# Cross-attention in two layers: the scores move to the head of a slot, and everything that prepares them is issued one slot earlier

## The chip, the cores and the metric

The kernel runs on one core of a Trainium2 chip. The metric is the device time of one execution in microseconds, as the median over several executions. A core has five engines that work side by side and meet through semaphores: TensorE (PE in the profile, with its weight loads on a row of their own, PEld), VectorE (DVE), ScalarE (ACT), GpSimd (POOL), and SyncE (SP), which here issues nearly all DMA transfers. Matrix products land in PSUM, which has 8 banks.

## The reference

Two layers of cross-attention run one after the other over `x` of shape (32, 256, 320), with a context of 77 tokens of width 512 for each of the 32 examples. There are 20 heads of width 16. The reference also has projections for further context tokens, but the context has exactly the 77 text tokens, so those parts work on nothing. For each layer what remains is:

```python
q = heads(x @ Wq)              # 32 x 20 x 256 x 16
k = heads(ctx @ Wk)            # 32 x 20 x 77 x 16
v = heads(ctx @ Wv)
s = einsum('bhqd,bhkd->bhqk', q, k) / sqrt(16)
p = softmax(s, axis=-1)
out = merge(einsum('bhqk,bhkd->bhqd', p, v))
x = out @ Wo + bo + x          # the second layer starts from this x
```

All of it is in float32.

## The kernel before

**Units and groups.** Two examples make a pair `p` (16 pairs). A pair in one layer is a unit `u` (32 units; `units_in_order` puts four pairs of layer 0 first and then alternates the layers). The 320 channels of a unit are handled in five groups `g` (`NG = 5`), each with four pairs of heads. `x`, `q` and the output are kept with channels on partitions and the rows of the example along the free axis.

**The steps of a unit.** `load_x` and `load_context` fetch the inputs through SP. `keys` and `keys_rest` project the context (psk) and GpSimd spreads the result over two masked copies, `kT`, of which `maxima` reads. `queries` and `queries_rest` project x (psq); ScalarE copies the result out of PSUM, and SP copies `q0` to `q1`. `vals` projects a chunk of 128 context tokens (psv), and `place_vals` sends the rows by DMA to where a unit's `v` is wanted.

The softmax needs a maximum over the 77 keys for each query and head. `maxima(u, g)` (line 335, PSUM tiles psm) computes the products with queries on partitions, and VectorE reduces each of the four tiles (line 343, about 0.44 us each). When all five groups are done, `turn(u)` transposes the maxima (line 352) and sends them with eight small DMAs into spare rows of q0 and q1 (line 356). `scores(u, g)` (line 369, tiles pss) computes the products a second time with keys on partitions; the spare rows and `kM` subtract the maximum in the same matmul. ScalarE then takes the exponential of each of the four tiles into `pT` (line 375). `values(u, g)` multiplies `pT` with `v` (line 389, tile po), VectorE transposes the result (line 401), takes the reciprocal of the sums (line 405), GpSimd multiplies (line 410), and `turn_back` transposes into `oT` (line 424). `finish` and `finish_rest` project the five groups of `oT` with Wo (tiles psy) and add bias and x (line 431). In `finish`, the products over the first 256 channels, that is groups 0 to 3, come first (`main_channels`), those over the last 64, group 4, at the end (`last_channels`).

**The order of the work.** There is no scheduler: the order on each engine is the order in which the Python code issues the steps. The loop near line 462 places every step in a numbered slot. A unit starts its scores at slot `s = 5 u`, with one group per slot, so `scores(u, g)` stands in slot `s + g` and `values(u, g)` in slot `s + g + 1`. All other steps stand at fixed distances from `s`. Within a slot the steps are issued by kind, in the order of the tuple in line 506:

```python
order = ("load", "maxima", "turn", "scores", "values", "rest", "back", "full", "last")
```

So a slot in the middle of the run holds the maxima of one group of a later unit, the scores of one group of the present unit, the values of the group before, and one or two projections ("rest", "full", "last"). With 32 units there are 160 slots that hold scores. Every engine works through its part of that list strictly in this order, apart from weight loads, which can go ahead of matmuls.

**PSUM.** All tiles in PSUM come from one pool of eight banks with one tag (`bank`, line 103), handed out in turn: the ninth tile asked for gets the bank of the first. The first instruction that writes a tile waits until the last reader of the tile that had the bank eight places earlier is done. Maxima and scores ask for four banks each, values for one, `queries` and `finish` for four each, and the other projections for one or two.

Of the kernel before, what the change touches and what calls it, by code (L numbers as in the profile page):

```python
# [60 lines left out]
NG = 5  # L61
# [29 lines left out]
def xattn_kernel(ctx: ExitStack, tc: tile.TileContext, xT, cT, cP, weights, outT):  # L91
    nc = tc.nc
# [10 lines left out]
    def bank(name):  # L103
        return psum.tile([P, 512], F32, tag="bank", name=name)
# [3 lines left out]
    def load_x(p):  # L108
        x_sb = io.tile([P, NX], F32, tag="x", name=f"x_{p}", bufs=AHEAD + 3)
        nc.sync.dma_start(out=x_sb, in_=xT[p])  # L110
        xs[p] = x_sb

    def load_context(u):
        p = units[u][0]
        c_sb = cs[u] = io.tile([P, NKA, NB * L], F32, tag="c", name=f"c_{u}", bufs=3)
        nc.sync.dma_start(out=c_sb, in_=cP[:, p])
# [10 lines left out]
    def load_weights(layer, first, last, queue):  # L127
        a = PARTS[first][0]
        at, rows, width = PARTS[last]
        b = at + rows * width  # L130
        queue.dma_start(out=w_sb[layer]["all"][:, a:b], in_=weights[layer][:, a:b])
# [12 lines left out]
    for layer in range(2):  # L144
        for i in range(2):

            v = const.tile([P, HEADS // 2, 2, 2, HD], F32, name=f"stage_{layer}_{i}")
# [82 lines left out]
    def keys(u):  # L230
        p, layer = units[u]
        w, c_sb = w_sb[layer], cs[u]
        kR = st[u]["kr"] = work.tile([P, NG, L], F32, tag="kR", name=f"kR_{u}", bufs=2)
        st[u]["k"] = work.tile([P, 2, NG, L], F32, tag="kT", name=f"kT_{u}", bufs=3)
        for t in range(2):
            ps = bank(f"psk_{u}_{t}")
            for kc in range(NKA):
                by_columns(
                    ps[:, 0 : 2 * L],
                    w["k"][:, kc, t * P : (t + 1) * P],  # L240
                    c_sb[:, kc, :],
                    start=(kc == 0),
                    stop=(kc == NKA - 1),
                )
            nc.scalar.copy(kR[:, 2 * t : 2 * t + 2].rearrange("p g k -> p (g k)"), ps[:, 0 : 2 * L])  # L245
        mask_keys(u, 0, 4)

    def keys_rest(u):

        p, layer = units[u]  # L250
        w, c_sb = w_sb[layer], cs[u]
        ps = bank(f"psk_{u}_2")
        for kc in range(NKA):
            for i in range(4):
                b, m = i // 2, i % 2
                nc.tensor.matmul(  # L256
                    ps[32 * i : 32 * i + 32, 0:L],
                    w["k"][:, kc, 2 * P + 32 * m : 2 * P + 32 * m + 32],
                    c_sb[:, kc, b * L : (b + 1) * L],
                    start=(kc == 0),  # L260
                    stop=(kc == NKA - 1),
                )
        nc.scalar.copy(st[u]["kr"][:, 4], ps[:, 0:L])
        mask_keys(u, 4, 5)

    def queries(u):
        p, layer = units[u]
        w = w_sb[layer]
        q0, _ = st[u]["q"] = [
            work.tile([P, NX], F32, tag=f"q{e}", name=f"q{e}_{u}", bufs=3) for e in range(2)  # L270
        ]
        ps = [[bank(f"psq_{u}_{t}_{b}") for b in range(NB)] for t in range(2)]
        last_channels(ps, w["q2"], xs[p], start=True, stop=False)
        main_channels(ps, w["q"], xs[p], start=False, stop=True)
        for g in range(4):
            nc.scalar.copy(of_group(q0, g), ps[g // 2][g % 2][:, 0:S])  # L276

    def queries_rest(u):
        p, layer = units[u]
        w = w_sb[layer]  # L280
        q0, q1 = st[u]["q"]
        ps = bank(f"psq_{u}_2")
        project_rest(ps, w["q"], w["q22"], xs[p])
        nc.scalar.copy(of_group(q0, 4), ps[:, 0:S])
        nc.sync.dma_start(out=q1, in_=q0)
        less_keys(u)
# [41 lines left out]
    def maxima(u, g):  # L328
        q0, kT, mx = st[u]["q"][0], st[u]["k"], maxes[u % 2]
        q = of_group(q0, g)  # L330
        ps = [bank(f"psm_{u}_{g}_{j}") for j in range(4)]
        for c in range(S // P):
            for j in range(4):
                r = slice(32 * j, 32 * j + 32)
                nc.tensor.matmul(  # L335
                    ps[j][:, c * 2 * L : (c + 1) * 2 * L],
                    q[r, c * P : (c + 1) * P],
                    kT[r, :, g, :],
                    start=True,
                    stop=True,  # L340
                )
        for j in range(4):
            nc.vector.tensor_reduce(  # L343
                mx[:, 2 * g : 2 * g + 2, 2 * j : 2 * j + 2],
                ps[j][:, : 4 * L].rearrange("p (c e k) -> p c e k", e=2, k=L),
                AX.X,
                ALU.max,
            )

    def turn(u):  # L350
        mT = work.tile([P, 2 * NG * 32], F32, tag="mT", name=f"mT_{u}", bufs=2)
        nc.vector.transpose(mT, maxes[u % 2].rearrange("p k i -> p (k i)"))
        for e in range(2):
            q = st[u]["q"][e].rearrange("(j i) n -> i j n", i=32)[HD * (1 - e)]
            for a in range(P // 32):
                nc.sync.dma_start(  # L356
                    out=q.rearrange("j (k a n) -> a j k n", a=P // 32, n=32)[a],
                    in_=mT[32 * a + e : 32 * a + 8 : 2].rearrange("j (k n) -> j k n", n=32),
                )
# [77 lines left out]
    def finish(u):  # L437
        w = w_sb[units[u][1]]
        ps = [[bank(f"psy_{u}_{t}_{b}") for b in range(NB)] for t in range(2)]
        main_channels(ps, w["o"], st[u]["o"], start=True, stop=False)  # L440
        last_channels(ps, w["o2"], st[u]["o"], start=False, stop=True)
        for g in range(4):
            add(u, g, ps[g // 2][g % 2])

    def finish_rest(u):
        p, layer = units[u]
        w = w_sb[layer]
        ps = bank(f"psy_{u}_2")
        project_rest(ps, w["o"], w["o22"], st[u]["o"])
        add(u, 4, ps)  # L450
        if layer == 1 and u < NU - 1:
            nc.sync.dma_start(out=outT[p], in_=xs[p])
        st[u].clear()
# [4 lines left out]
    def at(slot, where, step):  # L458
        place.setdefault((slot, where), []).append(step)

    made = [0, 0]
    for u, (p, layer) in enumerate(units):
        s = NG * u
        if layer == 0 and u > 0:
            at(s - 14, "load", lambda p=p: load_x(p))
        if u > 0:
            at(s - 12, "load", lambda u=u: load_context(u))
        at(s - 8 if u else s - 9, "rest", lambda u=u: keys(u))
        at(s - 9, "last", lambda u=u: queries(u))
        at(s - 7, "rest", lambda u=u: keys_rest(u))  # L470
        need = range(p * NB * L // P, ((p + 1) * NB * L - 1) // P + 1)
        when = s - 6
        for i in need:
            if i < made[layer]:
                at(when, "full", lambda u=u, i=i: place_vals(u, i))
                continue
            at(when - 3, "load", lambda layer=layer, i=i: load_chunk(layer, i))
            at(when, "full", lambda layer=layer, i=i: vals(layer, i))
            at(when, "full", lambda u=u, i=i: place_vals(u, i))
            made[layer] += 1  # L480
            when = s - 5
        at(s - 5, "rest", lambda u=u: queries_rest(u))
        for g in range(NG):
            at(s - 6 + g, "maxima", lambda u=u, g=g: maxima(u, g))
            at(s + g, "scores", lambda u=u, g=g: scores(u, g))
            at(s + g + 1, "values", lambda u=u, g=g: values(u, g))
            at(s + g + 1, "back", lambda u=u, g=g: turn_back(u, g))
        at(s - 2, "turn", lambda u=u: turn(u))
        if u < NU - 2:
            at(s + NG + 1, "full", lambda u=u: finish(u))  # L490
            at(s + NG + 3, "rest", lambda u=u: finish_rest(u))
        else:

            slot = NG * NU - (u == NU - 2)
            at(slot, "full", lambda u=u: finish(u))
            at(slot, "last", lambda u=u: finish_rest(u))


    at(-10, "load", lambda: load_weights(0, "v", "v", nc.scalar))
    at(-4, "load", lambda: load_weights(0, "o", "b", nc.sync))  # L500
    at(1, "load", lambda: load_weights(1, "k", "k", nc.sync))
    at(2, "load", lambda: load_weights(1, "q", "q22", nc.sync))
    at(3, "load", lambda: load_weights(1, "v", "v", nc.sync))
    at(4, "load", lambda: load_weights(1, "o", "b", nc.sync))

    order = ("load", "maxima", "turn", "scores", "values", "rest", "back", "full", "last")
    for slot in range(min(s for s, _ in place), max(s for s, _ in place) + 1):
        for where in order:
            for step in place.get((slot, where), ()):
# [96 lines left out]
```

## Time and profile before

| | |
|---|---|
| median of 3 runs | 984.96 us (984.57 to 988.63) |
| profiled execution, its own time | 986.19 us |
| its span, from the first to the last instruction | 984.4 us |
| granted TensorE clock, mean | 0.995 |
| busy: TensorE | 968.2 us |
| busy: VectorE, ScalarE, GpSimd | 566.7, 430.1, 240.9 us |

A timeline row gives the start in us from the start of the span, the time from the first start to the last end, engine, line and operation, the tile written and the tiles read, the shapes, and how many instructions were merged into the row. In brackets stands how long the engine was idle before it and what ended that. Rows of matmuls overlap: the end of a matmul is modelled, so distances are read from start to start. TensorE shows two records for each float32 matmul of the program, so the 8 matmuls of a group of maxima, scores or values are 16 records. "Idle before" on the row of weight loads (PEld) is not idle time of TensorE, which may be busy with matmuls meanwhile.

### The profile page before, as it was taken

The page shows a single profiled execution, that of the slowest core. Times are in us where ns is not written, and L with a number is a line of the kernel's source. Part 1 is how long each engine was busy: PE and PEld are TensorE (multiplying, and loading weights), DVE is VectorE, ACT ScalarE, POOL GpSimd, SP SyncE. Part 2 cuts the span into 40 slices and gives each one's busy share as a digit, 9 for nine tenths or more (in the row PEclk, how much of TensorE's full clock was granted, in tenths as well). Part 3 has the DMA queues.
Part 4 walks back from the last instruction along what each step waited for, and adds up shares of the span by engine and source line. Part 5 has one row for each costly group of instructions (what it writes and reads, how often), then busy time and mean ns, then how long its engine had stood idle before and what let it go on. Part 6 is the DMA issues. An engine that isn't in the chain of part 4 may idle for free.

```text
span 984.4 us, 43943 instructions
## 1 busy us (share of the span) xinstructions
PE 968.2 (98%) x19664; PEld 597.3 (61%) x19664; DVE 566.7 (58%) x1316; ACT 430.1 (44%) x937; POOL 240.9 (24%) x364
## 2 busy tenths in 40 slices
PE   7899999999999999999999999999999999999988
PEld 4566665666665666665666666666656666656644
DVE  2466555665555655556655556655556655556554
ACT  1354444444444444444544444543444444444443
POOL 3132221322212322212312213322223222123211
PEclk9999999999999999999999999999999999999999
DMA  6450222212132311323212232311323122231111
GB/s 216 165 174 21 92 80 97 70 62 72 64 123 71 121 54 50 107 81 123 63 51 85 70 124 71 104 44 60 123 81 118 33 67 70 70 108 48 50 57 55
DMA packets 53949, 83.59 MB, mean 85 GB/s; under 512 B 15556, under 2 KB 35652, under 8 KB 53762
## 3 DMA queue, kind: packets, MB, share of 16 engines
q1 hardware_dynamic: 53330, 78.96, 24.0%
q8 instruction: 154, 2.52, 1.0%
q10 hardware_dynamic: 432, 1.84, 0.5%
q14 instruction: 33, 0.27, 0.1%
HBM read 35.39 MB, written 10.49 MB: 47 GB/s over the span
## 4 chain that ended last, share of the span: by engine, by line
PE 97%; DMA 1%; DVE 1%; SPq 1%; POOL 0%; issue 0%; ACT 0%; DVEq 0%; POOLq 0%
PE po L389 16%; PE psy L173 15%; PE psq L173 15%; PE pss L369 14%; PE psm L335 12%; PE psv L173 9%; PE psk L173 7%; PE psq L212 4%; PE psy L212 4%; PE psk L256 2%; SPq L356 1%; DMA w<-in_w_dram 1%; DVE max L343 0%; DMA q<-mT 0%; POOL kT L219 0%
## 5 line engine op out<-in xcount | busy, mean ns | idle before, releaser
L375 ACT ACTIVATE pT<-pss 77x512 f32<-77x512 f32 x640 | 326.8, 590 | 210.4 <-PE pss L369 210.4
L343 DVE TENSOR_REDUCE max<-psm 128x4 f32<-128x308 f32 x640 | 260.6, 469 | 197.4 <-PE psm L335 194.0
L410 POOL TENSOR_TENSOR normal<-turned,inv 128x256 f32<-128x256 f32 x160 | 99.2, 620 | 684.5 <-DVE inv L405 684.5
L369 PE MATMUL pss<-q,kM 32*77 32x256 f32 x2560 | 170.9, 377 | 4.5 <-DMA q<-mT 4.5
L389 PE MATMUL po<-pT,v 77*32 77x256 f32 x2560 | 173.1, 388 | 1.3 <-DVE max L343 1.3
L173 PE MATMUL psy<-oT,w 128*32 128x256 f32 (+1 forms) x3072 | 149.2, 380 | 0.0
L173 PE MATMUL psq<-x,w 128*32 128x256 f32 (+1 forms) x3072 | 149.2, 379 | 0.0
L276 ACT COPY q<-psq 128x256 f32<-128x256 f32 x128 | 47.6, 372 | 205.9 <-PE psq L173 202.1
L401 DVE STREAM_TRANSPOSE turned<-po 128x512 f32<-128x512 f32 x160 | 113.3, 708 | 38.4 <-PE po L389 35.4
L424 DVE STREAM_TRANSPOSE oT<-normal 128x256 f32<-128x256 f32 x160 | 71.3, 445 | 109.4 <-POOL normal L410 109.4
L335 PE MATMUL psm<-kT,q 32*128 32x154 f32 x2560 | 129.4, 314 | 1.2 <-POOL kT L219 1.2
L335 PEld LDWEIGHTS psm<-kT,q 32*128 32x128 f32 x2560 | 92.2, 183 | 57.0 <-issue 34.9
L389 PEld LDWEIGHTS po<-pT,v 77*32 77x32 f32 x2560 | 67.4, 109 | 89.9 <-DVE max L343 58.7
L173 PEld LDWEIGHTS psq<-x,w 128*32 128x32 f32 (+1 forms) x3072 | 85.4, 108 | 57.2 <-issue 13.6
L173 PEld LDWEIGHTS psy<-oT,w 128*32 128x32 f32 (+1 forms) x3072 | 82.2, 109 | 61.2 <-issue 13.2
L369 PEld LDWEIGHTS pss<-q,kM 32*77 32x77 f32 x2560 | 102.2, 142 | 24.5 <-issue 6.8
L219 POOL TENSOR_SCALAR kT<-kR,masks 128x77 f32<-128x77 f32 (+1 forms) x128 | 96.7, 766 | 50.9 <-ACT kR L245 41.3
L431 DVE SCALAR_TENSOR_TENSOR x<-psy,w,x 128x256 f32<-128x256 f32 x160 | 68.6, 479 | 61.2 <-PE psy L173 56.5
L173 PE MATMUL psv<-w,cv 128*32 128x320 f32 x1232 | 93.5, 433 | 0.0
L173 PE MATMUL psk<-c,w 128*32 128x154 f32 x2048 | 75.0, 298 | 5.8 <-DMA w<-in_w_dram 5.8
L173 PEld LDWEIGHTS psk<-c,w 128*32 128x32 f32 x2048 | 67.0, 111 | 12.9 <-DMA w<-in_w_dram 5.8
L173 PEld LDWEIGHTS psv<-w,cv 128*32 128x32 f32 x1232 | 41.1, 110 | 40.6 <-issue 2.2
(25 smaller groups left out, 349.1 us busy)
## 6 DMA issues: line engine op xcount, KB each, us to landing
q<-q SPq DMA_DIRECT2D x32, 640.0 KB
x<-in_xT_dram SPq DMA_DIRECT2D x16, 640.0 KB
c<-in_cP_dram SPq DMA_DIRECT2D x32, 308.0 KB
cv<-in_cT_dram SPq DMA_DIRECT2D x38, 256.0 KB
out_dram<-x SPq DMA_DIRECT2D x15, 640.0 KB
v<-stage SPq DMA_DIRECT2D x26, 192.5 KB
q<-mT SPq DMA_DIRECT2D x256, 5.0 KB
w<-in_w_dram ACTq DMA_DIRECT2D x2, 640.0 KB
```

What stands on the lines that cost most here:

```text
L173: nc.tensor.matmul(out[m : m + 32], lhsT[:, m : m + 32], rhs, **flags)
L212: nc.tensor.matmul(ps[r, 0:S], lhsT, rhs, start=(kc == 0), stop=(kc == 2))
L219: nc.gpsimd.tensor_scalar_mul(kT[:, e, g0:g1], kR[:, g0:g1], masks[:, e : e + 1])
L335: nc.tensor.matmul(ps[j][:, c * 2 * L : (c + 1) * 2 * L], q[r, c * P : (c + 1) * P], kT[r, :, g, :], start=True, stop=True,)
L343: nc.vector.tensor_reduce(mx[:, 2 * g : 2 * g + 2, 2 * j : 2 * j + 2], ps[j][:, : 4 * L].rearrange("p (c e k) -> p c e k", e=2, k=L), AX.X ...
L369: nc.tensor.matmul(ps[j][:L, e * S : (e + 1) * S], kM[r, e, g, :], q[r, :], start=True, stop=True,)
L375: nc.scalar.activation(st[u]["p", g][j][:L], ps[j][:L], AF.Exp, scale=SCALE)
L389: nc.tensor.matmul(po[32 * j : 32 * j + 32, e * S : (e + 1) * S], vpad[:L, b, pair, e].rearrange("p a d -> p (a d)"), pT[j][:L, e * S : (e ...
L401: nc.vector.transpose(turned[:, 0 : 2 * S], po)
L410: nc.gpsimd.tensor_tensor(normal.rearrange("p q e d -> p e q d"), outs, inv.unsqueeze(3).broadcast_to([P, 2, S // 32, HD]), ALU.mult,)
L424: nc.vector.transpose(of_group(st[u]["o"], g), normal)
L431: nc.vector.scalar_tensor_tensor(x, ps[:, 0:S], w_sb[layer]["b"][:, 0, t : t + 1], x, ALU.add, ALU.add)
```

## The change

Two things are changed. In a slot, scores are now issued first, ahead of the maxima and `turn`. And every step that prepares scores (loads, keys, queries, vals, maxima, `turn`) and `finish` of the units up to the last two is placed one slot earlier relative to the scores and values. Steps that prepare scores keep their distances among themselves; `finish(u)` moves from the slot after the unit's last values into the same slot, behind them and behind their `turn_back`. The two last units' `finish` stays where it was.

```diff
     for u, (p, layer) in enumerate(units):
         s = NG * u
         if layer == 0 and u > 0:
-            at(s - 14, "load", lambda p=p: load_x(p))
+            at(s - 15, "load", lambda p=p: load_x(p))
         if u > 0:
-            at(s - 12, "load", lambda u=u: load_context(u))
-        at(s - 8 if u else s - 9, "rest", lambda u=u: keys(u))
-        at(s - 9, "last", lambda u=u: queries(u))
-        at(s - 7, "rest", lambda u=u: keys_rest(u))
+            at(s - 13, "load", lambda u=u: load_context(u))
+        at(s - 9 if u else s - 10, "rest", lambda u=u: keys(u))
+        at(s - 10, "last", lambda u=u: queries(u))
+        at(s - 8, "rest", lambda u=u: keys_rest(u))
         need = range(p * NB * L // P, ((p + 1) * NB * L - 1) // P + 1)
-        when = s - 6
+        when = s - 7
...
-            when = s - 5
-        at(s - 5, "rest", lambda u=u: queries_rest(u))
+            when = s - 6
+        at(s - 6, "rest", lambda u=u: queries_rest(u))
         for g in range(NG):
-            at(s - 6 + g, "maxima", lambda u=u, g=g: maxima(u, g))
+            at(s - 7 + g, "maxima", lambda u=u, g=g: maxima(u, g))
             at(s + g, "scores", lambda u=u, g=g: scores(u, g))
             at(s + g + 1, "values", lambda u=u, g=g: values(u, g))
             at(s + g + 1, "back", lambda u=u, g=g: turn_back(u, g))
-        at(s - 2, "turn", lambda u=u: turn(u))
+        at(s - 3, "turn", lambda u=u: turn(u))
         if u < NU - 2:
-            at(s + NG + 1, "full", lambda u=u: finish(u))
-            at(s + NG + 3, "rest", lambda u=u: finish_rest(u))
+            at(s + NG, "full", lambda u=u: finish(u))
+            at(s + NG + 2, "rest", lambda u=u: finish_rest(u))
...
-    at(-10, "load", lambda: load_weights(0, "v", "v", nc.scalar))
-    at(-4, "load", lambda: load_weights(0, "o", "b", nc.sync))
+    at(-11, "load", lambda: load_weights(0, "v", "v", nc.scalar))
+    at(-5, "load", lambda: load_weights(0, "o", "b", nc.sync))
...
-    order = ("load", "maxima", "turn", "scores", "values", "rest", "back", "full", "last")
+    order = ("load", "scores", "maxima", "turn", "values", "rest", "back", "full", "last")
```

The chunk loads stand three slots ahead of `when` and move with it.

## The prediction

> **What bounds the kernel now.** I read the page first: busy times, then the chain that ended last.
>
> ```profile
> span 984.4 us, 43943 instructions
> PE 968.2 (98%) x19664; PEld 597.3 (61%) x19664; DVE 566.7 (58%) x1316; ACT 430.1 (44%) x937; POOL 240.9 (24%) x364
> PE 97%; DMA 1%; DVE 1%; SPq 1%; POOL 0%; issue 0%; ACT 0%; DVEq 0%; POOLq 0%
> ```
>
> TensorE is the bound, and the table of stages says how completely: from 100 to 900 us it is busy for 800.00 of 800.00 us at clock 1.00. So in the steady part there is no idle time to win. All that an order can do there is leave TensorE idle. What can be won lies in the first 45 and the last 45 us.
>
> Second, the timeline of one steady slot, TensorE alone, then ScalarE.
>
> ```profile
> 422.64 0.81 PE L335 MATMUL psm<-kT,q 32*128 32x154 f32 x16
> 423.27 1.07 PE L369 MATMUL pss<-q,kM 32*77 32x256 f32 x16
> 424.27 1.07 PE L389 MATMUL po<-pT,v 77*32 77x256 f32 x16
> 425.15 1.48 PE L212 MATMUL psq<-x,w 128*32 128x256 f32 x24
> 426.56 0.81 PE L335 MATMUL psm<-kT,q 32*128 32x154 f32 x16
> ```
>
> Read the starts, since ends overlap: maxima (M) to scores (S) 0.63 us, S to values (V) 1.00 here (0.97 in most slots: 418.51 to 419.48), V to the projection 0.88, that one to the next M 1.41. Nothing is late. From M to V takes 1.60 us.
>
> Third, who waits for whom around V and around the exponentials.
>
> ```profile
> L375 ACT ACTIVATE pT<-pss x640: 582/592/598, 40.2 to 968.8; 77x512 f32<-77x512 f32 x160
> ...
> 424.39 2.04 ACT L375 ACTIVATE pT<-pss 77x512 f32<-77x512 f32 x4 [1.18 <-PE pss L369]
> ```
>
> Four exponentials follow each S: the first starts 1.12 us after S (423.27 to 424.39) and takes 0.59, the others 0.5 apart. V of this slot reads exponentials of the slot before, so today nobody in the slot needs them soon.
>
> Last, both ends of the run.
>
> ```profile
> 37.30 0.67 PE L369 MATMUL pss<-q,kM 32*77 32x256 f32 x8 [0.23 <-DMA q<-mT]
> 39.55 0.67 PE L369 MATMUL pss<-q,kM 32*77 32x256 f32 x8 [1.57 <-DMA q<-mT]
> 40.15 2.79 PE L212 MATMUL psq<-x,w 128*32 128x256 f32 x24
> ...
> 952.95 0.67 PE L369 MATMUL pss<-q,kM 32*77 32x256 f32 x8 [1.00 <-DMA q<-mT]
> 955.35 1.15 PE L369 MATMUL pss<-q,kM 32*77 32x256 f32 x8 [1.72 <-DMA q<-mT]
> 956.42 1.93 PE L389 MATMUL po<-pT,v 77*32 77x256 f32 x16
> ```
>
> Here scores wait for the maxima that `turn` sends by DMA, and the rows after the wait run slowly (2.79 us where the same 24 take 1.48 at 425.15): the granted clock is 0.78 from 36.2 to 43.8 us and 0.80 from 944.7 to 962.
>
> **The change, part by part.** No instruction is added or removed: projections, loads, maxima, `turn` and `finish` keep their order among themselves, and S and V come one slot later against all of them. In a slot the order M, S, V, projection becomes S, M, V, projection.
>
> *The bank that V takes.* All PSUM tiles come from one ring of 8 banks. In a slot M takes 4, S takes 4 and V is the ninth, so V takes the first bank of whichever came first. Before, that is M's first bank, released by VectorE's first maximum (0.44 us long). After, it is S's first bank, released by ScalarE's first exponential of the same slot. The waits in the program of the changed kernel say so: V's first matmul waits for ScalarE alone, at the count that this slot's first exponential sets, in each of the 152 slots (1 to 152) that hold S, M and V. S and M share slots 0 to 152; slot 0 has no V.
>
> Price, from S's start. S now follows a projection, V or `finish` instead of M. The rows for that are in the tail: S at 949.85 behind the projection at 948.44 (gap 1.41, as for M, so the start of a slot does not move), first exponential at 951.03, that is 1.18 (S behind M: 1.12). With 0.59 it ends at 1.77. Handing a bank back costs about 0.06: the maximum at 60.15 takes 0.44, and V's weights start at 60.65. So V starts at 1.83. Without the wait it could start earlier: S to the next operation takes 1.03 at most (949.85 to 950.88, where V follows), M to a 128-row operation 0.74 (14.90 to 15.64), together 1.77 at most, so the exponential comes last either way. Against 1.60 before, each slot gets 0.23 longer: 152 x 0.23 = **35.0 us**. Bounds: with 1.12 as S has it behind M, 0.17 a slot, 25 us; with 1.18 and as much again as the 0.06 of the handover, 0.29 a slot, 44 us. I take 0.23, because S in the new place has the tail's neighbours. V's own length (0.88) and the projection behind it stay; its first bank is S's second, whose exponential ends 0.5 after the first, 2.33 after S, while it starts at 1.83 + 0.88 = 2.71: hidden by V.
>
> *What is queued behind the wait.* On TensorE everything. On VectorE: the maxima start 0.82 after M, so about 1.74 after S (M 0.92 after S, by S's own pitch), and end at 3.4, then transpose 0.72, reciprocal 0.25, GpSimd's multiply 0.62 with about 0.2 of handing over, transpose back 0.45, ending near 5.6. A slot lasts at least 2.71 + 1.41 = 4.12, so the next maximum is wanted at 5.9 or later: nothing is late. `turn` (0.51) and the last add of `finish_rest` (0.48) fall into one slot of about 4.7 us. `turn` pushes the chain to 6.2, the add fits while GpSimd multiplies, and the next maximum is wanted at 6.4: zero, with 0.1 x 32 = 3 us as the upper end.
>
> *`finish` one slot earlier against V.* It now follows V of its own unit's last group and needs that group's output only in its last 16 matmuls, which begin 3.57 us after its first (399.69 to 403.26). It starts at 2.71, they begin at 6.28, the output is there at 5.6 to 5.7. Cost 0, by a cover of 0.6 us; were it gone by as much again, 30 x 0.6 = 18 us.
>
> *Loads and queues.* x, context and chunk loads, the weights, the placing of v, the copies q1 and the 8 transfers of each `turn` all move together, so SP's order changes only around `out` and nothing of it is waited for in the steady part (TensorE has no DMA wait between 45 and 940 us). GpSimd's masks (2.08, 0.94, 1.31 us) keep their places against the projections; the multiply behind them comes later in the slot, not earlier. 0.
>
> *Both ends.* Between the first `turn` and the first S there is now a whole slot more: M, the rest of the queries (1.41) and S, instead of M and S. S's first half starts near 38.4, its second waits from 38.9 to 39.55 for the DMA: 0.65 in place of 0.23 + 1.57, and without the slow stretch (1.3 us in the 24 matmuls, 0.3 behind them, 0.4 ahead of S). Gain 3.2, at least 1.2 if the clock drops all the same. In the tail one pair S and V (2.0 us) moves into the time that is waited for the last `turn`; by hand I get the last half of S at 0.2 us later against the maxima than now, so the gain is 2.0 - 0.2 = 1.8; bounds 0 and 2.7 + 2.5 (the waits, and the slow rows behind them: 5.52 from 956.42 to 961.94 for what takes about 3.0). Sum of both ends -5.0, from -1.2 to -8.4.
>
> **Sum.** 984.4 + 35.0 - 5.0 = 1014.4 us of span. The profiled execution took 986.19 us with its 984.4 of span; the median of the three runs is 984.96, 1.2 below that execution. 984.96 + 30.0 gives about **1015**.
>
> A rule that speaks against the change more loudly: the page "TensorE: Matmul & The Clock Gate" of the Trainium skill ("A second HAM failure mode: psum-queue depth-cycling") tells of a kernel whose bank cycling left TensorE idle for moments so often that its clock kept falling. In this trace V waited 0.81 us at 946.7 for a bank, and the 24 matmuls behind it took their usual 1.48. By the page, as an estimate, every tenth of the work at half clock would add some 98 us; by the row, nothing; I take the row.
>
> **Rivals.**
>
> *Not slower: the exponential is in time.* V would then start at about 1.55 after S if M follows S at S's own pitch (S's last four at 0.71, 0.22 more to M, 0.39 to M's last four, 0.24 to V), 0.05 earlier than now: 984.96 - 152 x 0.05 - 5.0 = 972. It decides where the first exponential is done 0.23 us earlier after S than the tail shows. Against it: 592 ns at a spread of 582 to 598, and three tail slots with the same 1.18 (949.85 to 951.03, 961.94 to 963.12, 966.20 to 967.38).
>
> *VectorE falls behind as well.* If a late output holds up the last matmuls of `finish` by 0.6 in 30 units, 18 us more: 1033. For it: VectorE's chain is now longer than the shortest slots. Against: those are followed by the longest one.
>
> *The clock falls.* A slow stretch as at 956.42 costs 2.5 us; one per unit (31) would give 1015 + 78 = 1093. For it: both waits for DMA were followed by one. Against: idle times of 0.81 and 0.52 (at 60.6) were not.
>
> **How the numbers follow.** Three runs spread by 0.4%, so about 0.5% (4.9 us) is what can be told from no change: 980.0 to 989.9. Chances: the bank wait alone 0.87; VectorE too 0.06; the clock 0.02; not slower 0.05, of which faster 0.03 and same 0.02 (half the wait hidden, price nearly met by both ends). The likeliest case's bounds: 25 - 8 = +17 (1002) and 44 + 3 - 1 = +46 (1031); the ends of that are unlikely together, and 8 in 10 lie in 1004 to 1026. Slower 0.95.
>
> **What would show it.** Right: V's group idle before it "<-ACT pT" in some 150 places, 0.15 to 0.3 us each where TensorE's idle is counted, V 1.83 after S, TensorE's busy share down to about 95%, its waits for q<-mT at the start shorter. Wrong: V earlier than 1.65 after S; waits on VectorE at `finish`; a granted clock below 0.98 in the steady part.

## The result and the profile after

The changed kernel takes 1012.62 us (median of 4 runs, 1011.93 to 1014.82) where the kernel before takes 985.69 us in the runs beside it. The ratio is 1.0272, with a 95% interval from 1.0244 to 1.0300: 2.7% slower. The forecast was 1015, with a range from 1004 to 1026. The profiled execution took 1014.82 us with a span of 1013.0, so spans compare as 1013.0 with 984.4: 28.6 us more.

The page of the changed kernel, its busy times and the chain that ended last:

```profile
span 1013.0 us, 43950 instructions
PE 970.6 (96%) x19664; PEld 610.8 (60%) x19664; DVE 552.8 (55%) x1316; ACT 430.9 (43%) x937; POOL 240.9 (24%) x364
PE 88%; ACT 9%; DVE 1%; issue 1%; DMA 1%; POOL 0%; SPq 0%; DVEq 0%; POOLq 0%
```

TensorE's work is the same (970.6 us against 968.2), and its share has fallen. ScalarE, which had 0% of the chain before, now has 9% of it. The steady part shows where: from 100 to 900 us TensorE was busy for all 800.00 us before. After the change the table of stages has (busy time of each engine, clock, DMA share, GB/s):

```profile
100.00:900.00 800.00, 774.18 (x15892) 491.84 (x15888) 444.85 (x1058) 346.88 (x756) 190.60 (x283) 1.00 0.23 77
```

The clock is 1.00 as before. 25.8 us are idle, and they are cut into small pieces. One steady slot, TensorE's timeline and then ScalarE's:

```profile
431.74 1.10 PE L369 MATMUL pss<-q,kM 32*77 32x256 f32 x16
432.67 0.70 PE L335 MATMUL psm<-kT,q 32*128 32x154 f32 x16
433.57 1.07 PE L389 MATMUL po<-pT,v 77*32 77x256 f32 x16 [0.20 <-ACT pT L375]
434.46 1.48 PE L212 MATMUL psq<-x,w 128*32 128x256 f32 x24
...
432.92 2.05 ACT L375 ACTIVATE pT<-pss 77x512 f32<-77x512 f32 x4 [0.62 <-PE pss L369]
```

Scores (S) start at 431.74, the maxima (M) 0.93 later, and the values (V) at 433.57, which is 1.83 after S. Before, M to V took 1.60. The first exponential starts 1.18 after S, and with its 0.59 it ends at 433.51, 0.06 ahead of V. The table of waits counts this over the run (total us, times, longest):

```profile
PE po L389 <- ACT pT L375: 29.6, 148, 0.5
```

Over all slots the medians are 0.925 from S to M and 0.901 from M to V, together 1.826 us, which is 0.226 more than the usual 1.60. Before, 35 of the slots took 1.63, so the price is better taken from the means of the steady slots, 1.828 and 1.607: 0.221 more in each of 152 slots, 33.6 us. The rest, 28.6 - 33.6 = -5.0 us, is what the two ends gained. At the start the scores' second half now waits 0.42 us for the DMA of the maxima, where the two halves waited 0.23 + 1.57, and the rows behind it run at full speed:

```profile
38.54 0.67 PE L369 MATMUL pss<-q,kM 32*77 32x256 f32 x8
39.64 0.67 PE L369 MATMUL pss<-q,kM 32*77 32x256 f32 x8 [0.42 <-DMA q<-mT]
40.13 0.70 PE L335 MATMUL psm<-kT,q 32*128 32x154 f32 x16
40.97 5.68 PE L173 MATMUL psq<-x,w 64*32 64x256 f32 x96
```

The granted clock between 36.2 and 43.8 us is 1.00 where it was 0.78. The queries at 40.97 pay for the same banks as V does elsewhere. There is no V yet in that slot, so they follow the maxima. Each of their four banks becomes free behind one of the four exponentials, and they take 5.61 us to the next scores where they usually take 4.59.

In the tail one long wait remains, and slow rows behind it:

```profile
981.36 0.67 PE L369 MATMUL pss<-q,kM 32*77 32x256 f32 x8
983.76 0.67 PE L369 MATMUL pss<-q,kM 32*77 32x256 f32 x8 [1.73 <-POOL normal L410]
985.36 1.75 PE L369 MATMUL pss<-q,kM 32*77 32x256 f32 x16
987.04 1.93 PE L389 MATMUL po<-pT,v 77*32 77x256 f32 x16
```

The second half of these scores waits for several semaphores. The view names a step on GpSimd as the last of them; the same wait is listed for the DMA of the maxima in the kernel before. From 987.04 to 992.64 the rows are about twice as long as usual. Only the profiled execution is known in such detail; its mean clock was 0.997, and the other three runs had 1.00 and spans of 1009.9 to 1010.7 us.

### The profile page after: what moved, and what is told of

It is laid out like the page before. It is cut to its first block, busy times and chain, and to the rows that moved or that the text cites. A ratio compares the mean times of both kernels' runs of the same rounds, so it can differ in the third digit from the quotient of the medians.

```text
span 1013.0 us, 43950 instructions
## 1 busy us (share of the span) xinstructions
PE 970.6 (96%) x19664; PEld 610.8 (60%) x19664; DVE 552.8 (55%) x1316; ACT 430.9 (43%) x937; POOL 240.9 (24%) x364
## 3 DMA queue, kind: packets, MB, share of 16 engines
q10 hardware_dynamic: 432, 1.84, 0.5%
## 4 chain that ended last, share of the span: by engine, by line
PE 88%; ACT 9%; DVE 1%; issue 1%; DMA 1%; POOL 0%; SPq 0%; DVEq 0%; POOLq 0%
PE pss L369 17%; PE po L389 17%; PE psq L173 14%; PE psy L173 14%; ACT pT L375 9%; PE psv L173 8%; PE psk L173 7%; PE psy L212 4%; PE psq L212 4%; PE psk L256 2%; PE psm L335 1%; DMA w<-in_w_dram 1%; SPq L356 0%; DVE max L343 0%; POOL normal L410 0%
## 5 line engine op out<-in xcount | busy, mean ns | idle before, releaser
L369 PE MATMUL pss<-q,kM 32*77 32x256 f32 x2560 | 178.7, 392 | 2.2 <-POOL normal L410 1.7
L369 PEld LDWEIGHTS pss<-q,kM 32*77 32x77 f32 x2560 | 89.1, 142 | 76.5 <-issue 51.8
L335 PEld LDWEIGHTS psm<-kT,q 32*128 32x128 f32 x2560 | 107.9, 184 | 13.5 <-issue 1.7
L335 PE MATMUL psm<-kT,q 32*128 32x154 f32 x2560 | 114.4, 289 | 1.2 <-POOL kT L219 1.2
L431 DVE SCALAR_TENSOR_TENSOR x<-psy,w,x 128x256 f32<-128x256 f32 x160 | 66.1, 463 | 50.7 <-PE psy L173 50.2
```

Source lines behind the costliest of these rows:

```text
L335: nc.tensor.matmul(ps[j][:, c * 2 * L : (c + 1) * 2 * L], q[r, c * P : (c + 1) * P], kT[r, :, g, :], start=True, stop=True,)
L369: nc.tensor.matmul(ps[j][:L, e * S : (e + 1) * S], kM[r, e, g, :], q[r, :], start=True, stop=True,)
L431: nc.vector.scalar_tensor_tensor(x, ps[:, 0:S], w_sb[layer]["b"][:, 0, t : t + 1], x, ALU.add, ALU.add)
```

## Experiments

### The order inside a slot, put back

```diff
-    order = ("load", "scores", "maxima", "turn", "values", "rest", "back", "full", "last")
+    order = ("load", "maxima", "turn", "scores", "values", "rest", "back", "full", "last")
```

This is the changed kernel with everything still issued one slot further ahead.

> The changed kernel with only the order inside a slot put back: maxima and turn ahead of the scores, everything still one slot further ahead. Theory (the loss is the order in the slot, through the bank that values take): M to V is 1.60 us again and no value waits for an exponential, so the 152 x 0.225 us = 34 us are gone and the gain at both ends stays: about 980 us, 0.990 to 0.997 of before. Rival (the loss comes from issuing things one slot further ahead, or from finish in the slot of its last values): it stays near 1012.

It took 978.29 us (978.06 to 978.46, 6 runs). The ratio to before is 0.9899 (0.9872 to 0.9927), so it lies 1% below the kernel before, with an interval clear of 1, and 3.4% below the changed kernel. TensorE is busy for 800.00 of the 800 us from 100 to 900 again, and M to V takes 1.60. In the tail, what is left of the waits for the last `turn` is this:

```profile
948.98 0.67 PE L369 MATMUL pss<-q,kM 32*77 32x256 f32 x8
950.24 0.67 PE L369 MATMUL pss<-q,kM 32*77 32x256 f32 x8 [0.60 <-DMA q<-mT]
950.85 1.07 PE L389 MATMUL po<-pT,v 77*32 77x256 f32 x16
```

The wait is 0.60 us in place of 1.00 + 1.72, and the values behind it take 1.07 where they took 1.93. So the loss is in the order inside the slot, and the slot of lead by itself is a gain: 976.5 of span against 984.4, 7.9 us in the profiled executions. Part of it is that no slow rows follow the wait here.

### The order inside a slot alone

```diff
 # the kernel before, with only this line changed
-    order = ("load", "maxima", "turn", "scores", "values", "rest", "back", "full", "last")
+    order = ("load", "scores", "maxima", "turn", "values", "rest", "back", "full", "last")
```

> The kernel before with only the order inside a slot changed: scores ahead of the maxima and turn, nothing issued further ahead. Theory: the steady slots lose the same 0.225 us (153 slots, 34 us), and both ends lose what the slot ahead gives the whole change: the first scores stand one slot nearer to their maxima, so the start waits longer for the DMA than before, some 1 to 3 us. About 985 + 34 + 1 = 1020 us, above the whole change (1012.6) by what the maxima-first kernel lies below the one before (7 us). Rival (lead and order act on each other in the steady part): away from 1020 by more than 4 us.

It took 1026.04 us (1024.85 to 1026.91), ratio 1.0369 (1.0337 to 1.0401), 6 us more than expected. The rival's condition was met (more than 4 us away from 1020), but not in the steady part of which it spoke. There the loss is the same: 774.53 of 800 us busy, S to M 0.925 and M to V 0.901 in the median. The error was in the ends, which lose 39.7 - 33.6 = 6.1 us instead of 1 to 3. In the tail the scores wait 2.16 + 1.82 us for the DMA, and behind that every row is slow up to `finish`:

```profile
986.87 0.67 PE L369 MATMUL pss<-q,kM 32*77 32x256 f32 x8 [2.16 <-DMA q<-mT]
989.37 1.15 PE L369 MATMUL pss<-q,kM 32*77 32x256 f32 x8 [1.82 <-DMA q<-mT]
990.45 1.93 PE L389 MATMUL po<-pT,v 77*32 77x256 f32 x16
992.31 2.00 PE L369 MATMUL pss<-q,kM 32*77 32x256 f32 x16
...
1003.71 2.00 PE L369 MATMUL pss<-q,kM 32*77 32x256 f32 x16
1005.65 1.93 PE L389 MATMUL po<-pT,v 77*32 77x256 f32 x16
...
1014.62 4.66 PE L173 MATMUL psy<-oT,w 128*32 128x256 f32 x96
```

The granted clock from 980 to 1010 us is 0.66, and 1.00 again from 1008.5 to 1024. From 990.45 to 1005.65 there are four pairs of V and S at 3.8 us each, where a pair takes 2.03 at full speed. So the four versions are: neither change 984.4 us of span, lead alone 976.5, order alone 1024.1, both 1013.0. The lead is worth 7.9 us with the maxima first and 11.1 with the scores first; the order costs 36.5 to 39.7.

### Which exponential holds the bank: the order of the four

```diff
-        for j in range(4):
+        for j in (1, 0, 2, 3):
             nc.scalar.activation(st[u]["p", g][j][:L], ps[j][:L], AF.Exp, scale=SCALE)
```

> The changed kernel with the four exponentials of a slot issued in the order 1, 0, 2, 3, so that the first bank of the scores is read second. Theory: values wait for that bank's reader, which now ends 0.49 us later, so V starts 2.32 us after S in place of 1.83 and 152 x 0.49 = 74 us are added: about 1087 us. Rival (values wait for ScalarE for another reason, such as the data of the slot before): no change, 1012.

It took 1014.57 us (ratio 1.0287, 1.0240 to 1.0335). That is close to the rival's number, but not for its reason. In this program V's first matmul waits for the count that the exponential of the second tile sets, which now stands first. So the pool does not hand out banks strictly in turn, as the kernel was described above. By the waits of this program, it hands out the bank whose last reader was issued first, and when the readers are exchanged V takes the other bank. The timeline is that of the changed kernel (S, M, V, and the exponentials on ScalarE):

```profile
433.48 1.10 PE L369 MATMUL pss<-q,kM 32*77 32x256 f32 x16
434.40 0.70 PE L335 MATMUL psm<-kT,q 32*128 32x154 f32 x16
435.32 1.07 PE L389 MATMUL po<-pT,v 77*32 77x256 f32 x16 [0.22 <-ACT pT L375]
...
434.68 2.05 ACT L375 ACTIVATE pT<-pss 77x512 f32<-77x512 f32 x4 [0.63 <-PE pss L369]
```

V starts 1.84 after S, 0.017 later than in the changed kernel in the median; over 152 slots that is 2.6 us. The run left the theory standing without testing it, so the next one delays the release in a way that no exchange of banks can go around.

### The first bank read twice

```diff
+    twice = const.tile([P, 512], F32, name="twice")
...
+        nc.scalar.activation(twice[:L], ps[0][:L], AF.Exp, scale=SCALE)
         for j in range(4):
             nc.scalar.activation(st[u]["p", g][j][:L], ps[j][:L], AF.Exp, scale=SCALE)
```

> The changed kernel with the first of a slot's exponentials issued twice, the first time into a tile that nobody reads, so that the first bank is released 0.49 us later and nothing else on TensorE is touched. Exchanging the order of the exponentials did not move the release, because values take the bank whose last reader was issued first, whichever that is; here it is delayed for any order. Theory: V starts 2.32 us after S in place of 1.83; 152 x 0.49 = 74 us more than the changed kernel, about 1087 us. Rival (the wait only names ScalarE and V is held by something else): no change, 1013.

It took 1086.03 us (1085.92 to 1086.94), ratio 1.0979 (1.0940 to 1.1018), against 1087 expected. S to M is 0.925 as before and M to V 1.384, 0.48 more than in the changed kernel; 152 x 0.48 = 73 us. A slot:

```profile
430.68 0.59 ACT L375 ACTIVATE twice<-pss 77x512 f32<-77x512 f32 x1 [0.62 <-PE pss L370]
431.17 2.03 ACT L377 ACTIVATE pT<-pss 77x512 f32<-77x512 f32 x4
...
430.43 0.70 PE L336 MATMUL psm<-kT,q 32*128 32x154 f32 x16
431.81 1.07 PE L391 MATMUL po<-pT,v 77*32 77x256 f32 x16 [0.68 <-ACT pT L377]
```

V now waits for the exponential that is issued second (431.17 + 0.59 = 431.76), where in the run before it waited for the one issued first. Both times it is the last reader of the bank that comes free first. So it is the bank that holds V, and not the first exponential as such. ScalarE's total work is far from its limit here (507.0 us busy of 1084.1). What moves the end of the run is only when the first of S's banks comes free, and it does so one for one.

### The first exponential halved

```diff
-        for j in range(4):
+        pT0 = st[u]["p", g][0]
+        nc.gpsimd.memset(pT0[:L, 256:], 1.0)
+        nc.scalar.activation(pT0[:L, :256], ps[0][:L, :256], AF.Exp, scale=SCALE)
+        for j in range(1, 4):
             nc.scalar.activation(st[u]["p", g][j][:L], ps[j][:L], AF.Exp, scale=SCALE)
```

> The changed kernel with the first of a slot's four exponentials cut to half of its columns (GpSimd fills the other half with ones, so that half of those probabilities is left out). It should take about 0.38 in place of 0.59 us and free the bank 0.21 us earlier, which is ahead of the time at which TensorE is through with S and M (0.92 + 0.74 = 1.66 us). Theory (of the 0.225 us that a slot lost, 0.165 are the wait and 0.06 the dearer neighbours S, M, V in place of M, S, V): V 1.66 after S, 152 x 0.165 = 25 us less than the changed kernel: about 988 us. Rival (the whole 0.225 is the wait): 152 x 0.225 = 34 us less, about 978.

This kernel leaves out half of the probabilities of the first of the four tiles and has ones in their place. It took 985.62 us (983.43 to 993.34, 10 runs), ratio 0.9983 (0.9952 to 1.0014). The halved exponential takes 0.380 us in all 160 slots, and the wait is gone from TensorE:

```profile
436.85 0.70 PE L335 MATMUL psm<-kT,q 32*128 32x154 f32 x16
437.56 1.07 PE L392 MATMUL po<-pT,v 77*32 77x256 f32 x16
438.44 2.29 PE L173 MATMUL psk<-c,w 128*32 128x154 f32 x64
```

M to V is 0.709 in the median, S to V 0.925 + 0.709 = 1.634. So of the 0.226 us that a slot loses, 1.826 - 1.634 = 0.192 is the wait (29.2 us over 152 slots) and 1.634 - 1.600 = 0.034 the order of the neighbours (5.2 us). The theory's split was 0.165 and 0.06. It took M to V from a neighbouring row (0.74, maxima ahead of another operation); the real pair is 0.03 cheaper. The total lies between the two expected numbers and nearer to the theory's.

### Values ahead of the maxima

```diff
-    order = ("load", "scores", "maxima", "turn", "values", "rest", "back", "full", "last")
+    order = ("load", "scores", "values", "maxima", "turn", "rest", "back", "full", "last")
```

> The changed kernel with values ahead of the maxima: S, V, M. Values then take a bank that the slot before has freed, and the fourth tile of the maxima takes the scores' first bank, some 1.9 us after S, when it is free. Theory (the neighbours on TensorE cost time of their own): no wait for an exponential, but S to V 1.03, V to M 1.00 and M to the projection 0.74 make 2.77 us in place of 2.71 with the wait and 2.49 before: 152 x 0.06 = 9 us more than the changed kernel, about 1021. Rival (only the wait costs): about 978.

It took 1029.11 us (1026.98 to 1033.20), ratio 1.0419 (1.0377 to 1.0460), with 1025.1 of span in the profile, 8 us above the expected time. The wait is gone altogether, and the kernel is slower than with it:

```profile
432.83 1.10 PE L369 MATMUL pss<-q,kM 32*77 32x256 f32 x16
433.87 1.07 PE L389 MATMUL po<-pT,v 77*32 77x256 f32 x16
434.87 0.81 PE L335 MATMUL psm<-kT,q 32*128 32x154 f32 x16
435.60 2.36 PE L173 MATMUL psv<-w,cv 128*32 128x320 f32 x32
```

S to V 1.03, V to M 1.00 and M to the projection 0.74 are the expected 2.77 us. Each projection behind M instead of V is also 0.02 longer (1.433 for 1.411, 4.478 for 4.456), some 3 us in all, and with 152 x 0.06 = 9 us that gives the 12 us of span above the changed kernel. All of it is counted as busy time: TensorE is busy for 800.00 of 800 us. The remaining 4 us of the median are in runs that were not profiled; the kernel before also came out higher in them (990.18 us).

### One slot more of lead

The maxima-first kernel with loads, projections, maxima and `turn` one slot further ahead again. `finish` stays in the slot of the last values, since it can't be earlier.

```diff
-        at(s - 10, "last", lambda u=u: queries(u))
+        at(s - 11, "last", lambda u=u: queries(u))
...
-            at(s - 7 + g, "maxima", lambda u=u, g=g: maxima(u, g))
+            at(s - 8 + g, "maxima", lambda u=u, g=g: maxima(u, g))
...
-        at(s - 3, "turn", lambda u=u: turn(u))
+        at(s - 4, "turn", lambda u=u: turn(u))
```

> The maxima-first kernel with projections, maxima and turn one slot further ahead again (two more than before). What is left of DMA waits in the maxima-first kernel is one of 0.9 us in the tail; the steady part has none. Theory (the lead only pays where scores wait for the last turn): 0.9 us less at most, 977.4 to 978.5 us. Rival (more lead moves more scores and values into the tail, where four exponentials bound a slot): 979 to 981.

It took 1025.11 us (1024.30 to 1025.63), ratio 1.0360 (1.0332 to 1.0387). Both expectations missed by 45 us. The edit tore apart two steps that had shared a slot: `finish` and `queries`. With them together, 4.6 us of query projections on TensorE cover VectorE's four adds on the four banks of `finish`. Apart, the next slot begins right behind `finish` (rows of TensorE, and below them VectorE's adds; the psy row is `finish`):

```profile
419.23 4.66 PE L173 MATMUL psy<-oT,w 128*32 128x256 f32 x96
423.82 0.81 PE L335 MATMUL psm<-kT,q 32*128 32x154 f32 x16
424.45 1.84 PE L369 MATMUL pss<-q,kM 32*77 32x256 f32 x16
...
430.04 1.07 PE L389 MATMUL po<-pT,v 77*32 77x256 f32 x16 [0.60 <-DVE max L343]
...
423.50 1.66 DVE L431 SCALAR_TENSOR_TENSOR x<-psy,w,x 128x256 f32<-128x256 f32 x4 [3.87 <-PE psy L173]
```

The scores take over banks of `finish` and wait for the adds (the DVE row, which ends at 425.16) inside their 16 records: 1.78 us to V in place of 0.97. VectorE, now late, holds up V one slot later (1.64 in place of 0.97). That is 0.81 + 0.67 us in each of 30 units, 44 us, of the 46.0 by which the span is above the maxima-first kernel (1022.5 and 976.5). In the steady part the rows around the two separated projections add another 0.16 us to a unit, some 5 us, and the ends take about 3 back.

### `finish` left where it was

```diff
-            at(s + NG, "full", lambda u=u: finish(u))
-            at(s + NG + 2, "rest", lambda u=u: finish_rest(u))
+            at(s + NG + 1, "full", lambda u=u: finish(u))
+            at(s + NG + 3, "rest", lambda u=u: finish_rest(u))
```

This is the changed kernel in all else.

> The changed kernel with finish and finish_rest put back one slot later, so that they no longer follow the unit's last values in the same slot. Theory (finish in the same slot costs nothing, since its last matmuls want the last group's output 0.6 us after it is there): 1011 to 1014, as the changed kernel. Rival (part of the loss is finish waiting for that output): up to 18 us less, 995 to 1008.

It took 1026.52 us (1025.66 to 1026.90), ratio 1.0373 (1.0342 to 1.0405). It is neither the same nor faster but about 1.4% slower than the changed kernel. The cause is that of the run before: without the queries behind it, the banks of `finish` are wanted again too soon. Here it is the maxima that take them:

```profile
112.35 1.25 PE L335 MATMUL psm<-kT,q 32*128 32x154 f32 x16
112.60 2.04 ACT L375 ACTIVATE pT<-pss 77x512 f32<-77x512 f32 x4 [5.23 <-PE pss L369]
113.39 1.64 DVE L343 TENSOR_REDUCE max<-psm 128x4 f32<-128x308 f32 x4 [0.63 <-PE psm L335]
113.53 1.07 PE L389 MATMUL po<-pT,v 77*32 77x256 f32 x16
...
111.10 1.66 DVE L431 SCALAR_TENSOR_TENSOR x<-psy,w,x 128x256 f32<-128x256 f32 x4 [3.64 <-PE psy L173]
```

The four adds of `finish` end at 112.76, and the last records of the maxima start just behind them. M to V is 1.18 us in this slot of each unit and 0.95 in the next, against 0.90: 30 x 0.33 = 10 us. The rows around the two separated projections add 0.18 us to a unit, another 5. The span is only 10.8 us longer (1023.8 against 1013.0), mostly because here the tail has a wait of 1.00 us and no slow rows, where the profiled execution of the changed kernel has both 1.73 us and slow rows. So moving `finish` along with the projections saved time, and its own dependence on the last group cost none: nothing in the changed kernel waits there.

## Why the prediction was right

The predicted price of a slot was 0.23 us in 152 slots, 35.0 us; it measured 0.221 in the mean and 33.6. S to V was forecast at 1.83 us and is 1.826 in the median. Point by point:

- *The bank that V takes.* Right in place, engine and size. The 1.18 us from the scores to the first exponential were read from rows in the tail where S already had its new neighbours, and hold in the steady slots (431.74 to 432.92). The rule behind it was wrong, though harmless here: banks go by the order in which their last readers were issued, not strictly in turn, as the exchange of exponentials showed.
- *The exponential comes last.* Right: V is ready 1.634 after S without it, which is below the 1.77 that was stated as the most. The prediction did not say how the 0.226 divides; it is 0.192 for the wait and 0.034 for the order S, M, V on TensorE.
- *VectorE behind V.* Right: VectorE's reductions were forecast from 1.74 us after S and start 1.65 after it (at 433.39 in the slot shown), and no wait for VectorE of any size appears in the steady part. That rival is out for this kernel, though one slot's difference for `finish` makes it real.
- *`finish` at cost 0.* Right. Missing was why it has to move: it must keep the queries behind it. The cover named was for the output of the last group; the one that mattered was for the adds.
- *Both ends.* -5.0 forecast, -5.0 measured, but that it comes out to the tenth is partly luck. At the start the second half of the scores waits 0.42 (0.65 forecast) and the clock does not drop, as expected; the 1.02 us that the first queries lose to the exponentials are not in the forecast. In the tail one wait for the DMA and a slow stretch remain in the profiled execution, while the other three runs, 2.3 to 3.1 us shorter at a clock of 1.00, seem to have none.
- *The clock.* The Trainium skill ("TensorE: Matmul & The Clock Gate", "A second HAM failure mode: psum-queue depth-cycling") tells of a kernel whose clock kept changing because its bank cycling left TensorE idle for moments. No such fall shows here. Some 150 idle pieces of 0.2 us, and 0.68 us in the run with the bank read twice, left the granted clock at 1.00. While TensorE is at work, the clock falls only behind DMA waits at the start and in the tail, and not behind each of them.
- *Not slower.* The rival asked for the first exponential 0.23 us earlier. The run with the halved exponential gave 0.21 and came out at 0.9983 (0.9952 to 1.0014) of before, with both ends' gain in it. So an earlier exponential does remove the wait, but the rival's 972 was too low: V then starts 1.634 after S and not 1.55, which is 0.034 later than before and not 0.05 earlier.

The median came 2.4 us below the forecast. The steady part accounts for 1.4 and the ends for nothing; the rest lies in the medians of before and after against their profiled executions.

## What to carry to other kernels

In a software pipeline that shares a small pool of PSUM banks, the order inside a slot decides who releases the bank that the next tile takes. Work out that release from start, duration and handover before exchanging two steps, even if neither needs the other's data. A shift that moves everything ahead by a slot can gain at both ends, but steps that cover each other's bank releases (here `finish` and the queries) have to move together. When two changes come in one edit, run each alone: here one was worth 8 us and the other cost 37.

## What was not expected of the hardware

After the DMA waits in the tail, the clock can stay low for long although TensorE is at work. With the scores first and no lead, two waits of 2.16 and 1.82 us were followed by 15 us in which each pair of V and S took 3.8 us instead of 2.03. TensorE was busy for 15.10 of the 15.10 us from 990.5 to 1005.6, and the granted clock was 0.50:

```profile
990.50:1005.60 15.10, 15.10 (x131) 5.86 (x128) 5.22 (x11) 8.18 (x16) 2.46 (x4) 0.50 0.01 1
```

In the kernel before, waits of 1.00 and 1.72 us were followed by about 5.5 slow microseconds. The maxima-first kernel, with one wait of 0.60 us, shows no slow stretch there. The length of the wait alone does not decide it: 1.73 us at the same place was followed by slow rows in the changed kernel, but not in the run with the exponentials exchanged:

```profile
986.67 0.67 PE L369 MATMUL pss<-q,kM 32*77 32x256 f32 x8 [1.73 <-POOL normal L410]
987.28 1.07 PE L389 MATMUL po<-pT,v 77*32 77x256 f32 x16
988.28 1.10 PE L369 MATMUL pss<-q,kM 32*77 32x256 f32 x16
```

What does decide it stays open. The six runs of the maxima-first kernel lie within 0.4 us, where those of before lie between 984 and 992. The clock goes with that spread: of the runs of before, one of 984.76 us had a mean clock of 0.998, one of 992.49 us 0.988. That the low clock of the slower ones lies in the tail is likely but not shown, since they were not profiled.
